# Graph layer 1 in a hand-written order: turned accumulation, 12 target blocks from kept rows instead of 16

## The chip, the cores and the metric

The kernel runs on one core of a Trainium2 chip. Its time is the device time of one execution in microseconds (us), and the number compared is the median of several executions. Before the change the median of 5 runs is 4278.44 us (4270.95 to 4283.33). The engines are named as in the profile: PE multiplies matrices (PEld loads its weights), DVE is the vector engine, ACT the scalar engine, POOL issues the indirect loads ("gathers"), and SP issues the other loads and stores.

## The reference

Four graph layers follow each other over 6250 nodes with 256 features and 100000 edges, sorted by target (`dst`); each ends in a residual and a layer norm. The change is in the second, layer 1. The reference, cut to it:

```
x = _layernorm(x + _L0_gnn_ref(x, edge_index, L0_gnn_W, L0_gnn_b), axis=-1)
x = _layernorm(x + _L1_gnn_ref(x, edge_index, L1_gnn_W1, ...), axis=-1)
x = _layernorm(x + _L2_gnn_ref(x, src, dst, edge_weight, ...), axis=-1)
x = _layernorm(x + _L3_gnn_ref(x, edge_attr_128, edge_index, ...), axis=-1)

def _L1_gnn_ref(h, edge_index, W1, b1, W2, b2, eps, gamma, beta):
    src, dst = (edge_index[0], edge_index[1])
    agg = jax.ops.segment_sum(h[src], dst, num_segments=h.shape[0])
    z = (1.0 + eps) * h + agg
    z = jax.nn.relu(z @ W1 + b1) @ W2 + b2
    r = z + h
    mu = jnp.mean(r, axis=-1, keepdims=True)
    var = jnp.mean(jnp.square(r - mu), axis=-1, keepdims=True)
    ln = (r - mu) * jax.lax.rsqrt(var + LN_EPS) * gamma + beta
    return jax.nn.relu(ln)
```

Targets are drawn as a square, so low node numbers receive many more edges than high ones.

## The kernel before

The nodes are cut into 49 blocks of 128 (`NB`), a block being a tile of 128 partitions x 256 features. The kernel runs in stages, one after the other: a preparation (edge lists and attention scores, 0 to 1020 us of the profiled span), layer 0 (to about 1570), layer 1 (1579.4 to 2317.6), layer 2 (to 3320) and layer 3 (to the end at 4279.5).

Sums over edges are matrix products. Layer 0 leaves each row of x as two halves whose sum is the row (512 values, 256 `hi` and 256 `lo`); most blocks' halves stay in the on-chip memory ("kept rows": `keep`, and `first_rows` for the first 20 blocks, loaded again from `rows`), and all are in the table `rows`. In layer 1 a target block gets its sum over edges in one of two ways.

*Near blocks*, 0 to 15 (`H1` = 16), use kept rows. There are four sweeps of four target blocks each, and each sweep goes over all 49 source blocks: 196 steps. A step makes the one-hot matrices of the edges between a source block and the four targets on DVE (`Pairs`, L1022 `od` by target, L974 through `one_hots` `os` by source), multiplies them on PE (L1284, into `ps_q`) to a 128 x 512 matrix of edge counts, which ACT copies out (L1287, `a_hi`). The next step's `use` multiplies the counts with the source block's kept rows, in eight matmuls of 256 columns (`sum_halves`, L985 and L986, two for each of four targets), which add up in `ps_acc`, laid out target node by feature.

*Far blocks*, 16 to 48, use gathers: 383 tiles of 128 edges, in 76 chunks of up to six. Each tile is a gather of 128 rows of 512 values on POOL (L979, `g`, 8 buffers), and two matmuls (L985, L986) with a one-hot matrix `cs` made on DVE add it to `ps_g`. The chunks are spread evenly over the steps by `want`.

Once a group of four blocks (`GRP`) has its sums, z = (1+eps)x + sum is formed on DVE (L1217), transposed on PE (L357) with a copy on ACT (L358), and `finish` follows: a first product into `ps_b` (L370) with bias and relu on ACT (`y_t`, L1226), the second product (L364), the two sums with b2 and x (L1232, L1233), a layer norm (L344 to L350), gamma and beta (L1235, L1236), relu and the outer residual (L1237), a second layer norm, and the store on SP (L376). A norm takes statistics on DVE (L344, L346), a root on ACT (L348), and a reciprocal and a two-scalar operation on DVE (L349, L350).

Layers 0 and 2 are written in an order fixed by hand (`manual_schedule`). Layer 1 is not: there the framework's scheduler decides the order of the instructions on each engine, while buffer counts bound how far one may run ahead of another.

The preparation loads, for each far block, two columns of the edge list through SP (into `idx_d` and `to`) and makes `loc_d`, the target's place within its block, on DVE. Layer 0's weight `w_raw` is loaded through SP.

Of the kernel before, what the change touches and what calls it, by code (L numbers as in the profile page):

```python
# [7 lines left out]
FT = mybir.dt.float32  # L8
# [42 lines left out]
S_TILES = sum(n for _, _, _, n in STRETCHES)  # L51
TS = NB * S_TILES
S_ROWS = -(-(S_TILES * P * NB + E) // P)
H0, H1, H2, H3 = 24, 16, 9, 3
SURE = 3.5


# [321 lines left out]
def one_plus(k, pool, eps, name):  # L379
    t = bcast_row(k, pool, eps, 1, name)  # L380
    k.nc.vector.tensor_scalar(t, t, 1.0, None, op0=OP.add)
    return t
# [561 lines left out]
def load_block(k, pool, table, b, name="xb", bufs=3):  # L944

    t = pool.tile([P, D], FT, name=name, bufs=bufs)
    n = rows_of(b)
    if n < P:
        k.nc.vector.memset(t, 0.0)
    k.nc.sync.dma_start(t[:n, :], table[b * P:b * P + n, :])  # L950
    return t
# [245 lines left out]
def direct_l1(k, pool, psum, a, rows_at, table, idx_d, loc_d, loc, rel, x_in, out_x):  # L1197


    nc = k.nc  # L1200
    w1 = weight(k, pool, a["L1_gnn_W1"], D, D, "w1")
    w2 = weight(k, pool, a["L1_gnn_W2"], D, D, "w2")
    b1 = column(k, pool, a["L1_gnn_b1"], DK, "b1")
    b2 = bcast_row(k, pool, a["L1_gnn_b2"], D, "b2")
    gamma = bcast_row(k, pool, a["L1_gnn_gamma"], D, "gamma")
    beta = bcast_row(k, pool, a["L1_gnn_beta"], D, "beta")
    eps1 = one_plus(k, pool, a["L1_gnn_eps"], "eps1")

    class Group:
        def __init__(self, b0, n):  # L1210
            self.b0, self.n, self.x = b0, n, {}
            self.z_t = pool.tile([P, DK, GRP * P], FT, name="z_t", bufs=2)

        def add(self, i, ps):
            x = self.x[i] = load_block(k, pool, x_in, self.b0 + i, name="x1", bufs=8)
            z = pool.tile([P, D], FT, name="z1", bufs=2)
            nc.vector.scalar_tensor_tensor(z, x, eps1, ps, op0=OP.mult, op1=OP.add)  # L1217
            transposed(k, self.z_t[:, :, i * P:(i + 1) * P], z)

        def finish(self):  # L1220
            n = self.n
            y_t = pool.tile([P, DK, GRP * P], FT, name="y_t", bufs=2)
            for o in range(DK):
                py = k.psum.tile([P, GRP * P], FT, name="ps_b")
                times_t(k, py[:, :n * P], w1, self.z_t[:, :, :n * P], o)
                nc.scalar.activation(y_t[:, o, :n * P], py[:, :n * P], AF.Relu, bias=b1[:, o:o + 1])  # L1226
            for i in range(n):
                b, x = self.b0 + i, self.x[i]
                pr = k.psum.tile([P, D], FT, name="ps_b")
                times(k, pr, y_t[:, :, i * P:(i + 1) * P], w2)  # L1230
                r = pool.tile([P, D], FT, name="r1", bufs=3)
                nc.vector.tensor_add(r, b2, pr)  # L1232
                nc.vector.tensor_add(r, r, x)  # L1233
                layernorm(k, pool, r, r)
                nc.vector.tensor_mul(r, r, gamma)  # L1235
                nc.vector.tensor_add(r, r, beta)  # L1236
                nc.vector.scalar_tensor_tensor(r, r, 0.0, x, op0=OP.max, op1=OP.add)  # L1237
                layernorm(k, pool, r, r)
                store_block(k, out_x, b, r)

    def far_blocks():
        for b0 in range(H1, NB, GRP):
            g = Group(b0, min(GRP, NB - b0))
            for i in range(g.n):
                b = b0 + i
                ps = psum.tile([P, D], FT, name="ps_g", bufs=2)
                for c0 in range(0, D_TILES[b], CHUNK):
                    m = min(CHUNK, D_TILES[b] - c0)
                    at = D_FIRST[b] + c0
                    s = pool.tile([P, CHUNK, P], F32R, name="cs", bufs=2)  # L1250
                    one_hots(k, s[:, :m, :], loc_d[:, at:at + m])
                    for j in range(m):
                        r = pool.tile([P, W0], FT, name="g", bufs=8)
                        gather(k, r, table, idx_d[:, at + j:at + j + 1])
                        sum_halves(k, ps, s[:, j, :], r, start=(c0 + j == 0), stop=(c0 + j == D_TILES[b] - 1))
                    yield
                g.add(i, ps)
            g.finish()

    far = far_blocks()  # L1260
    n_far = sum(-(-D_TILES[b] // CHUNK) for b in range(H1, NB))
    steps = [(d0, b) for d0 in range(0, H1, 4) for b in range(NB)]
    ones, done, sums = {}, [0], {}

    def open_step(i):
        d0, b = steps[i]
        ones[i] = Pairs(k, pool, b, d0, d0 + 4, loc, rel)

    open_step(0)

    def build(i):
        if i + 1 < len(steps):
            open_step(i + 1)
        d0, b = steps[i]
        p = ones.pop(i)


        pa = psum.tile([P, 4 * P], FT, name="ps_q", bufs=2)
        for m, t in enumerate(p.tiles):
            lo, hi = p.spans[t]  # L1280
            new = next((d for d in range(lo, hi) if p.of(d)[0] == t), hi)
            for d, e in ((lo, new), (new, hi)):
                if d < e:
                    nc.tensor.matmul(pa[:, (d - d0) * P:(e - d0) * P], p.by_source(t), p.by_target(t, d, e - d),  # L1284
                                     start=(m == 0), stop=(m == len(p.tiles) - 1 and e == hi))
        at = pool.tile([P, 4, P], F32R, name="a_hi", bufs=3)
        nc.scalar.copy(at.rearrange("p j s -> p (j s)"), pa)  # L1287
        return at

    def use(i, at):  # L1290
        d0, b = steps[i]
        if b == 0:
            sums[0] = psum.tile([P, 4, D], FT, name="ps_acc", bufs=1)
        for j in range(4):
            n = rows_of(b)
            sum_halves(k, sums[0][:, j, :], at[:n, j, :], rows_at(b)[:n, :], start=(b == 0 and j % 2 == 0),
                       stop=(b == NB - 1 and j % 2 == 1))
        want = (i + 1) * n_far // len(steps)
        while done[0] < want:
            next(far, None)  # L1300
            done[0] += 1
        if b == NB - 1:
            g = Group(d0, 4)
            for j in range(4):
                g.add(j, sums[0][:, j, :])
            g.finish()

    stages(len(steps), 1, build, use)
    for _ in far:
        pass  # L1310


def direct_l2(k, pool, a, hot, idx, loc, rel, scale, x_in, out_rows, out_x, si):
# [595 lines left out]
def prepare(k, a, table0, first, rec, placed, ends, idx_d, loc_d, bad):  # L1909
# [6 lines left out]
    with (  # L1916
# [11 lines left out]
        scatter = Scatter(k, r_s, addr, rec, "scatter")  # L1928
        scores = Scores(k, prep, ps, a["edge_attr_128"], a["L3_gnn_ew_W"], a["L3_gnn_ew_b"], a["L3_gnn_a_W"],
                        r_s[:, :, 3], scatter.columns)  # L1930
        w_raw = weight(k, prep, a["L0_gnn_W"], D, D, "w_raw")
        with tc.tile_pool(name="cols", bufs=1) as cols:
            none = cols.tile([P, TS // 49, 4], FT, name="none")
            for i, v in enumerate((float(NONE), -1.0, 0.0, 0.0)):
# [26 lines left out]
        with tc.tile_pool(name="score", bufs=1) as pool:  # L1961
# [17 lines left out]
            at(NB // 3 + 4, lambda: setattr(scores, "placed", Placed(k, pool, ps, slots, r_s, placed)))  # L1979


            w_t = pool.tile([P, DK, D], FT, name="w_t")
            bias = bcast_row(k, pool, a["L0_gnn_b"], D, "b_row")
            x_ts = {}
# [155 lines left out]
```

## Time and profile before

| | |
|---|---|
| median of 5 runs | 4278.44 us (4270.95 to 4283.33) |
| the profiled execution | 4281.38 us |
| its span | 4279.5 us |
| mean granted PE clock over the span | 0.926 |
| PE busy over the span | 3606.2 us (84%) |
| DVE busy | 2949.8 us (69%) |
| POOL busy | 2737.0 us (64%) |
| ACT busy | 1475.8 us (34%) |
| gathers of layer 1 (L979 with `idx_d`) | 383, 431.5 us busy, mean 1127 ns |

A line of instruction groups is read so: line, engine, operation, what is written `<-` what is read, the number of times, then busy us and mean ns of one, then the idle time of the engine before them and what ended it. "PEclk" is the clock granted to PE, as a share of its full speed. A busy time of PE is larger than the time that its matmuls keep it from others, since they overlap. A line of a timeline has start and duration in us, the engine, the line and the operation, and in brackets the idle time before it with its releaser; SPq is SP's queue.

### The profile page before, as it was taken

Reading aid. Unit: us, or ns where it says so; the run is one execution under the profiler, and the core shown is the slowest. Engines: PE = TensorE matmul, PEld = TensorE weight load, DVE = VectorE, ACT = ScalarE, POOL = GpSimd, SP = SyncE. Lnnn points to the kernel's source line nnn. Section 1 sums busy time; section 2 is a strip of 40 time slices with the busy share of each in tenths; the row PEclk is TensorE's granted clock in tenths of the full one; section 3 lists DMA queues with packets and bytes.
Section 4 is the critical chain, followed back from the end, with each engine's and each line's share of the span. In section 5 each row is a group of like instructions: output and inputs, shape, how many; then the busy total and the mean of one; then the engine's idle time right before and its main releaser. Section 6 shows DMA issues by size and latency. Waiting matters only on the chain. (4 is left out here: it accounts for less than half of the span.)

```text
span 4279.5 us, 70812 instructions
## 1 busy us (share of the span) xinstructions
PE 3606.2 (84%) x23978; PEld 2791.2 (65%) x23988; DVE 2949.8 (69%) x9234; ACT 1475.8 (34%) x3780; POOL 2737.0 (64%) x2685
## 2 busy tenths in 40 slices
PE   7999999984999988988886999999853777777676
PEld 4566666644999977766665777777532565666565
DVE  7787666544777758888887565565286777777775
ACT  1344333331333322222222111111343455555554
POOL 3765655676777757566663777777303777777774
PEclk9999999997999999899998999999997888888888
DMA  4233333325777775456563343343244445444443
GB/s 81 61 88 92 92 87 85 87 54 135 218 211 214 216 228 170 135 170 173 166 184 93 108 108 108 108 109 108 59 111 127 124 133 140 136 137 140 134 139 91
DMA packets 373432, 552.44 MB, mean 129 GB/s; under 512 B 88710, under 2 KB 265064, under 8 KB 372774
## 3 DMA queue, kind: packets, MB, share of 16 engines
q0 software_dynamic: 136064, 353.87, 30.3%
q1 hardware_dynamic: 236998, 193.96, 15.5%
q8 instruction: 193, 3.16, 0.3%
q14 instruction: 177, 1.45, 0.1%
HBM read 486.32 MB, written 62.09 MB: 128 GB/s over the span
## 5 line engine op out<-in xcount | busy, mean ns | idle before, releaser
L979 POOL DMA_INDIRECT g<-rows,idx_s x1032 | 1153.6, 1118 | 393.5 <-issue 239.6
L929 POOL DMA_INDIRECT rec<-r_s,addr x590 | 578.8, 981 | 337.5 <-ACT r_s L829 221.3
L979 POOL DMA_INDIRECT g<-x,idx_s x541 | 560.1, 1035 | 220.9 <-issue 74.3
L979 POOL DMA_INDIRECT g<-rows,idx_d x383 | 431.5, 1127 | 271.9 <-PE ps_g L986 160.6
L825 PE MATMUL ps_b<-ew_w,a_t 128*128 128x257 f32 x1564 | 548.4, 433 | 2.0 <-ACT a_t L815 2.0
L827 DVE SCALAR_TENSOR_TENSOR scr<-ps_b,a 128x256 bf16<-128x256 f32 x782 | 324.9, 422 | 255.8 <-PE ps_b L825 231.5
L1630 PE MATMUL ps_g<-g,s 128*128 128x257 f32 x1374 | 393.0, 454 | 0.0
L1130 PEld LDWEIGHTS <-od 128*128 128x128 bf16 x5947 | 349.2, 98 | 52.9 <-issue 19.8
L1630 PEld LDWEIGHTS ps_g<-g,s 128*128 128x128 f32 x1374 | 315.3, 233 | 59.1
L1138 PE MATMUL ps_g<-g,cs 128*128 128x256 f32 x1082 | 289.6, 394 | 48.6 <-DMA g<-x,idx_s 47.1
L829 ACT ACTIVATE r_s<-ps_b,half 128x1 f32<-128x1 f32 x782 | 201.0, 263 | 360.5 <-DVE scr L827 355.0
L1092 DVE TENSOR_SCALAR od<-iota,rel 128x128 bf16<-128x128 f16 (+9 forms) x780 | 249.4, 400 | 104.1 <-PE ps_q L1130 99.9
L974 DVE TENSOR_TENSOR os<-iota_row,loc_s 128x768 bf16<-128x768 f32 (+3 forms) x294 | 270.9, 921 | 70.6 <-PE ps_q L1284 60.0
L825 PEld LDWEIGHTS ps_b<-ew_w,a_t 128*128 128x128 f32 x1564 | 233.4, 188 | 97.1 <-ACT a_t L815 2.3
L1550 PE MATMUL ps_a<-ident,ep 128*128 128x128 f32 x833 | 163.9, 328 | 148.3 <-DVE ep L1539 89.1
L1133 ACT CAST a_hi<-ps_q 128x512 fp32r<-128x512 f32 x294 | 172.2, 586 | 330.0 <-PE ps_q L1130 319.9
L1133 ACT COPY a_hi<-ps_q 128x512 f32<-128x512 f32 x146 | 69.9, 479 | 593.0 <-PE ps_q L1130 573.4
L985 PE MATMUL ps_g<-g,cs 128*128 128x256 f32 x728 | 232.3, 336 | 46.8 <-DMA g<-rows,idx_d 45.5
L1138 PEld LDWEIGHTS ps_g<-g,cs 128*128 128x128 f32 x1082 | 186.8, 190 | 109.8 <-DMA g<-x,idx_s 89.1
L1287 ACT CAST a_hi<-ps_q 128x512 fp32r<-128x512 f32 x196 | 114.8, 586 | 380.2 <-PE ps_q L1284 379.9
L985 PE MATMUL ps_g<-first_rows,a_hi 128*128 128x256 f32 x980 | 245.7, 283 | 0.0
L986 PE MATMUL ps_g<-first_rows,a_hi 128*128 128x256 f32 x980 | 244.4, 282 | 0.0
(294 smaller groups left out, 8201.0 us busy)
## 6 DMA issues: line engine op xcount, KB each, us to landing
at<-in_edge_attr SPq DMA_DIRECT2D x65, 768.0 KB
edge_row<-node_row SPq DMA_DIRECT2D x49, 544.0 KB
xb<-x SPq DMA_DIRECT2D x144, 128.0 KB
g<-rows,idx_s POOLq DMA_INDIRECT x1032
xb<-in_x SPq DMA_DIRECT2D x96, 128.0 KB
x<-x SPq DMA_DIRECT2D x96, 128.0 KB
rows<-hl SPq DMA_DIRECT2D x47, 256.0 KB
rec<-r_s,addr POOLq DMA_INDIRECT x590
```

What stands on the lines that cost most here:

```text
L825: nc.tensor.matmul(z[:n_e, :], a_t[:, j * P:j * P + n_e], self.w, start=False, stop=True)
L827: nc.vector.scalar_tensor_tensor(scr[:n_e, :], z[:n_e, :D], 0.0, self.a[:n_e, :], op0=OP.max, op1=OP.mult, accum_out=s[:n_e, j:j + 1])
L929: s = nc.gpsimd.indirect_dma_start(out=self.table, out_offset=bass.IndirectOffsetOnAxis(ap=self.addr[:n, c:c + 1], axis=0), in_=self.rec[: ...
L974: k.nc.vector.tensor_tensor(dst, k.iota_row.unsqueeze(1).to_broadcast([P, n, P]), loc.unsqueeze(2).to_broadcast([P, n, P]), op=op)
L979: k.nc.gpsimd.indirect_dma_start(out=dst, out_offset=None, in_=table, in_offset=bass.IndirectOffsetOnAxis(ap=idx, axis=0))
L985: k.nc.tensor.matmul(out, lhs, row[:, :D].bitcast(F32R), start=start, stop=False)
L986: k.nc.tensor.matmul(out, lhs, row[:, D:2 * D].bitcast(F32R), start=False, stop=stop)
L1092: nc.vector.tensor_scalar(od[:, o:o + (hi - lo) * P], k.iota16[:, :(hi - lo) * P], rel[:, s + t:s + t + 1], None, op0=OP.is_equal)
L1130: nc.tensor.matmul(pa[:, j * P:(j + 1) * P], od[:, o:o + P], x[:, t, :], start=(m == 0), stop=(m == len(steps) - 1))
L1133: nc.scalar.copy(a[:, :n, :].rearrange("p j s -> p (j s)"), pa[:, :n * P])
L1138: nc.tensor.matmul(ps, a, row, start=start, stop=stop)
L1630: nc.tensor.matmul(ps, s[:, j, :], g[:, j, :D + 1], start=(j == 0), stop=False)
```

## The change

Layer 1 is written in a fixed order, its near blocks are fewer, and its accumulation is turned.

- `H1` goes from 16 to 12: three sweeps and 147 steps instead of 196. Target blocks 12 to 48 are gathered: 450 tiles in 88 chunks instead of 383 in 76. The preparation loads and prepares the edge lists of four more blocks.
- `ps_acc` is laid out feature by target node. The kept rows are the weights and `a_hi` the moving side: four matmuls of 512 columns a step in place of eight of 256. Near blocks need no z and no transposes: (1+eps)x is added in the accumulation by two small matmuls per block (at source blocks 26 to 29) with `scaled`, the identity times 1+eps, and ACT copies the sum straight to `z_t`. Their x is loaded at source block 18 (`xn`).
- Everything in the layer stands in `manual_schedule`. Iteration i makes the one-hots of step i+1, builds the counts of step i, does one or more pieces of waiting group work (the list `later`), multiplies step i-1, and then uses a chunk if one is due. A chunk's sums (`use_chunk`) are followed by the one-hots and gathers of the next chunk (`open_chunk`). Chunks are due over the first 137 of 148 iterations.
- A group's work is cut in pieces: `first` (first product), then pieces in which `second`, `sums`, `middle` and `end` of successive blocks overlap.
- In the norms gamma, beta and the normalising are folded into operations with one per-partition scalar and one tensor (`scalar_tensor_tensor`); the last normalising goes to ACT as y = r * rs - mean * rs, with a 128 x 1 product `less` on DVE.
- `g` has 11 buffers instead of 8, `ps_g` one instead of two, `ps_b` two.
- `w_raw` is loaded later, after the preparation's first loads.

The diff, without blank lines and with long removed stretches cut (they stand above):

```diff
@@ -51,7 +51,7 @@
 S_TILES = sum(n for _, _, _, n in STRETCHES)
 TS = NB * S_TILES
 S_ROWS = -(-(S_TILES * P * NB + E) // P)
-H0, H1, H2, H3 = 24, 16, 9, 3
+H0, H1, H2, H3 = 24, 12, 9, 3
 SURE = 3.5
@@ -1197,6 +1197,8 @@
 def direct_l1(k, pool, psum, a, rows_at, table, idx_d, loc_d, loc, rel, x_in, out_x):
     nc = k.nc
     w1 = weight(k, pool, a["L1_gnn_W1"], D, D, "w1")
     w2 = weight(k, pool, a["L1_gnn_W2"], D, D, "w2")
@@ -1205,72 +1207,123 @@
     gamma = bcast_row(k, pool, a["L1_gnn_gamma"], D, "gamma")
     beta = bcast_row(k, pool, a["L1_gnn_beta"], D, "beta")
     eps1 = one_plus(k, pool, a["L1_gnn_eps"], "eps1")
+    scaled = pool.tile([P, P], FT, name="scaled")
+    nc.vector.tensor_scalar(scaled, k.ident, eps1, None, op0=OP.mult)
+    later = []
     class Group:
         def __init__(self, b0, n):
-            self.b0, self.n, self.x = b0, n, {}
-            self.z_t = pool.tile([P, DK, GRP * P], FT, name="z_t", bufs=2)
-        def add(self, i, ps):
-            x = self.x[i] = load_block(k, pool, x_in, self.b0 + i, name="x1", bufs=8)
+            self.b0, self.n, self.x, self.r, self.ln, self.pr = b0, n, {}, {}, {}, {}
+            self.z_t = None
+        def inputs(self):
+            if self.z_t is None:
+                self.z_t = pool.tile([P, DK, GRP * P], FT, name="z_t", bufs=2)
+            return self.z_t
+        def load(self, i):
+            near = self.b0 < H1
+            self.x[i] = load_block(k, pool, x_in, self.b0 + i, name="xn" if near else "x1", bufs=4 if near else 8)
+        def turn(self, i, z):
+            transposed(k, self.inputs()[:, :, i * P:(i + 1) * P], z)
+        def first(self):
+            n = self.n
+            self.y_t = pool.tile([P, DK, GRP * P], FT, name="y_t", bufs=2)
+            for o in range(DK):
+                py = psum.tile([P, GRP * P], FT, name="ps_b", bufs=2)
+                times_t(k, py[:, :n * P], w1, self.z_t[:, :, :n * P], o)
+                nc.scalar.activation(self.y_t[:, o, :n * P], py[:, :n * P], AF.Relu, bias=b1[:, o:o + 1])
+        def second(self, i):
+            self.pr[i] = psum.tile([P, GRP * P], FT, name="ps_b", bufs=2)[:, :D]
+            times(k, self.pr[i], self.y_t[:, :, i * P:(i + 1) * P], w2)
+        def sums(self, i):
+            r = self.r[i] = pool.tile([P, D], FT, name="r1", bufs=3)
+            nc.vector.tensor_add(r, b2, self.pr.pop(i))
+            nc.vector.tensor_add(r, r, self.x[i])
+            self.ln[i] = spread(k, pool, r)
+        def middle(self, i):
+            r, (mv, rs) = self.r[i], self.ln[i]
+            nc.vector.reciprocal(rs, rs)
+            nc.vector.scalar_tensor_tensor(r, r, mv[:, 0:1], gamma, op0=OP.subtract, op1=OP.mult)
+            nc.vector.scalar_tensor_tensor(r, r, rs, beta, op0=OP.mult, op1=OP.add)
+            nc.vector.scalar_tensor_tensor(r, r, 0.0, self.x.pop(i), op0=OP.max, op1=OP.add)
+            self.ln[i] = spread(k, pool, r)
+        def end(self, i):
+            mv, rs = self.ln.pop(i)
+            nc.vector.reciprocal(rs, rs)
+            less = pool.tile([P, 1], FT, name="less1", bufs=3)
+            nc.vector.tensor_scalar(less, mv[:, 0:1], rs, -1.0, op0=OP.mult, op1=OP.mult)
+            y = pool.tile([P, D], FT, name="y1", bufs=2)
+            nc.scalar.activation(y, self.r.pop(i), AF.Identity, bias=less, scale=rs)
+            store_block(k, out_x, self.b0 + i, y)
+        def pieces(self):
+            def piece(m):
+                for f, lag in ((self.second, 0), (self.end, 3), (self.middle, 2), (self.sums, 1)):
+                    if 0 <= m - lag < self.n:
+                        f(m - lag)
+            return [self.first] + [lambda m=m: piece(m) for m in range(self.n + 3)]
+    def after(*fs):
+        later.extend(fs)
+    chunks = [(b, c0, min(CHUNK, D_TILES[b] - c0)) for b in range(H1, NB) for c0 in range(0, D_TILES[b], CHUNK)]
+    opened, far_group, far_sum = {}, {}, {}
+    def open_chunk(c):
+        b, c0, m = chunks[c]
+        at = D_FIRST[b] + c0
+        if c0 == 0:
+            i = (b - H1) % GRP
+            if i == 0:
+                far_group[b] = Group(b, min(GRP, NB - b))
+            far_group[b - i].load(i)
+        s = pool.tile([P, CHUNK, P], F32R, name="cs", bufs=2)
+        one_hots(k, s[:, :m, :], loc_d[:, at:at + m])
+        rows = []
+        for j in range(m):
+            rows.append(pool.tile([P, W0], FT, name="g", bufs=11))
+            gather(k, rows[-1], table, idx_d[:, at + j:at + j + 1])
+        opened[c] = s, rows
+    def use_chunk(c):
+        b, c0, m = chunks[c]
+        s, rows = opened.pop(c)
+        if c0 == 0:
+            far_sum[b] = psum.tile([P, D], FT, name="ps_g", bufs=1)
+        ps = far_sum[b]
+        for j in range(m):
+            sum_halves(k, ps, s[:, j, :], rows[j], start=(c0 + j == 0), stop=(c0 + j == D_TILES[b] - 1))
+        if c0 + m == D_TILES[b]:
+            i = (b - H1) % GRP
+            g = far_group[b - i]
             z = pool.tile([P, D], FT, name="z1", bufs=2)
-            nc.vector.scalar_tensor_tensor(z, x, eps1, ps, op0=OP.mult, op1=OP.add)
...
-    n_far = sum(-(-D_TILES[b] // CHUNK) for b in range(H1, NB))
+            nc.vector.scalar_tensor_tensor(z, g.x[i], eps1, far_sum.pop(b), op0=OP.mult, op1=OP.add)
+            after(lambda: g.turn(i, z))
+            if i == g.n - 1:
+                after(*g.pieces())
+        if c + 1 < len(chunks):
+            open_chunk(c + 1)
     steps = [(d0, b) for d0 in range(0, H1, 4) for b in range(NB)]
-    ones, done, sums = {}, [0], {}
+    ones, sums, near_group, made = {}, {}, {}, {}
     def open_step(i):
         d0, b = steps[i]
         ones[i] = Pairs(k, pool, b, d0, d0 + 4, loc, rel)
-    open_step(0)
     def build(i):
-        if i + 1 < len(steps):
-            open_step(i + 1)
         d0, b = steps[i]
         p = ones.pop(i)
@@ -1283,31 +1336,56 @@
                 if d < e:
                     nc.tensor.matmul(pa[:, (d - d0) * P:(e - d0) * P], p.by_source(t), p.by_target(t, d, e - d),
                                      start=(m == 0), stop=(m == len(p.tiles) - 1 and e == hi))
-        at = pool.tile([P, 4, P], F32R, name="a_hi", bufs=3)
-        nc.scalar.copy(at.rearrange("p j s -> p (j s)"), pa)
-        return at
-    def use(i, at):
+        at = made[i] = pool.tile([P, 4 * P], F32R, name="a_hi", bufs=3)
+        nc.scalar.copy(at, pa)
+    def use(i):
         d0, b = steps[i]
+        at, n = made.pop(i), rows_of(b)
         if b == 0:
-            sums[0] = psum.tile([P, 4, D], FT, name="ps_acc", bufs=1)
...
-            done[0] += 1
+            sums[0] = psum.tile([P, DK, 4 * P], FT, name="ps_acc", bufs=1)
+        acc = sums[0]
+        for o in range(DK):
+            for part in range(2):
+                row = rows_at(b)[:n, part * D + o * P:part * D + (o + 1) * P]
+                nc.tensor.matmul(acc[:, o, :], row.bitcast(F32R), at[:n, :], start=(b == 0 and part == 0),
+                                 stop=(b == NB - 1 and part == 1))
+        g = near_group.get(d0)
+        if b == 18:
+            g = near_group[d0] = Group(d0, 4)
+            for j in range(4):
+                g.load(j)
+        if 26 <= b < 30:
+            j = b - 26
+            for o in range(DK):
+                nc.tensor.matmul(acc[:, o, j * P:(j + 1) * P], g.x[j][:, o * P:(o + 1) * P], scaled, start=False,
+                                 stop=False)
         if b == NB - 1:
-            g = Group(d0, 4)
...
-        pass
+            for o in range(DK):
+                nc.scalar.copy(g.inputs()[:, o, :], acc[:, o, :])
+            after(*g.pieces())
+    with k.tc.manual_schedule():
+        open_step(0)
+        open_chunk(0)
+        done = 0
+        for i in range(len(steps) + 1):
+            if i + 1 < len(steps):
+                open_step(i + 1)
+            if i < len(steps):
+                build(i)
+            for _ in range(1 + len(later) // 5):
+                if later:
+                    later.pop(0)()
+            if i:
+                use(i - 1)
+            want = min(len(chunks), (i + 1) * len(chunks) // (len(steps) - 10))
+            while done < want:
+                use_chunk(done)
+                done += 1
+        while later:
+            later.pop(0)()
 def direct_l2(k, pool, a, hot, idx, loc, rel, scale, x_in, out_rows, out_x, si):
@@ -1928,7 +2006,6 @@
         scatter = Scatter(k, r_s, addr, rec, "scatter")
         scores = Scores(k, prep, ps, a["edge_attr_128"], a["L3_gnn_ew_W"], a["L3_gnn_ew_b"], a["L3_gnn_a_W"],
                         r_s[:, :, 3], scatter.columns)
-        w_raw = weight(k, prep, a["L0_gnn_W"], D, D, "w_raw")
         with tc.tile_pool(name="cols", bufs=1) as cols:
             none = cols.tile([P, TS // 49, 4], FT, name="none")
             for i, v in enumerate((float(NONE), -1.0, 0.0, 0.0)):
@@ -1979,6 +2056,7 @@
             at(NB // 3 + 4, lambda: setattr(scores, "placed", Placed(k, pool, ps, slots, r_s, placed)))
+            w_raw = weight(k, pool, a["L0_gnn_W"], D, D, "w_raw")
             w_t = pool.tile([P, DK, D], FT, name="w_t")
             bias = bcast_row(k, pool, a["L0_gnn_b"], D, "b_row")
             x_ts = {}
```

`spread(k, pool, x)` takes the statistics of a norm (DVE) and the root (ACT) and returns mean and root; the caller forms the reciprocal. In the changed file the lines of layer 1 are L1337 (counts), L1340 (`a_hi`), L1351 (accumulation), L1362 (`scaled`), L1366 (copies to `z_t`), L1312 (z of far blocks), L1248 and L1249 (`sums`), L1254 to L1257 (`middle`) and L1262 to L1266 (`end`).

More of the change, by code (lines that the diff above doesn't have):

```diff
@@ L1207, in direct_l1 @@
     eps1 = one_plus(k, pool, a["L1_gnn_eps"], "eps1")
+    scaled = pool.tile([P, P], FT, name="scaled")
+    nc.vector.tensor_scalar(scaled, k.ident, eps1, None, op0=OP.mult)
+    later = []
     class Group:
         def __init__(self, b0, n):
-            self.b0, self.n, self.x = b0, n, {}
-            self.z_t = pool.tile([P, DK, GRP * P], FT, name="z_t", bufs=2)
-        def add(self, i, ps):
-            x = self.x[i] = load_block(k, pool, x_in, self.b0 + i, name="x1", bufs=8)
-            z = pool.tile([P, D], FT, name="z1", bufs=2)
-            nc.vector.scalar_tensor_tensor(z, x, eps1, ps, op0=OP.mult, op1=OP.add)
-            transposed(k, self.z_t[:, :, i * P:(i + 1) * P], z)
@@ L1220, in finish @@
[L1220 to L1258, printed above, removed]
@@ L1260, in direct_l1 @@
-    far = far_blocks()
-    n_far = sum(-(-D_TILES[b] // CHUNK) for b in range(H1, NB))
+            self.b0, self.n, self.x, self.r, self.ln, self.pr = b0, n, {}, {}, {}, {}
[7 more added lines that the diff above has]
+            self.x[i] = load_block(k, pool, x_in, self.b0 + i, name="xn" if near else "x1", bufs=4 if near else 8)
@@ L1285, in build @@
                                      start=(m == 0), stop=(m == len(p.tiles) - 1 and e == hi))
-        at = pool.tile([P, 4, P], F32R, name="a_hi", bufs=3)
-        nc.scalar.copy(at.rearrange("p j s -> p (j s)"), pa)
-        return at
-    def use(i, at):
+        at = made[i] = pool.tile([P, 4 * P], F32R, name="a_hi", bufs=3)
+        nc.scalar.copy(at, pa)
+    def use(i):
         d0, b = steps[i]
+        at, n = made.pop(i), rows_of(b)
         if b == 0:
-            sums[0] = psum.tile([P, 4, D], FT, name="ps_acc", bufs=1)
[L1294 to L1300, printed above, removed]
-            done[0] += 1
-        if b == NB - 1:
-            g = Group(d0, 4)
-            for j in range(4):
-                g.add(j, sums[0][:, j, :])
-            g.finish()
@@ L1308, in direct_l1 @@
-    stages(len(steps), 1, build, use)
-    for _ in far:
-        pass
+            sums[0] = psum.tile([P, DK, 4 * P], FT, name="ps_acc", bufs=1)
[6 more added lines that the diff above has]
+        g = near_group.get(d0)
```

## The prediction

> **What bounds the kernel now.** The chain of waits on the page is of no help (every share in it is 0%), so I went by stages: first the busy time of each engine in windows whose borders are the first and last instruction of a layer, then the groups and waits of layer 1 alone, then the timeline at its two ends.
>
> ```profile
> core 0: us, PE busy (x) PEld busy (x) DVE busy (x) ACT busy (x) POOL busy (x), PEclk, DMA share, GB/s
> 1020.00:1570.00 550.00, 545.96 (x5918) 533.03 (x5915) 377.00 (x857) 202.94 (x393) 381.10 (x337) 1.00 0.70 213
> 1579.40:2317.60 738.20, 619.10 (x3944) 485.12 (x3954) 599.97 (x1894) 178.47 (x372) 431.49 (x383) 0.91 0.56 161
> 2318.00:3055.00 737.00, 683.61 (x5215) 559.97 (x5215) 430.42 (x1100) 99.40 (x218) 560.10 (x541) 0.99 0.39 106
> ```
>
> The middle line is layer 1, the only stage whose inner work changes: 738.2 us. No engine is full. PE is busy 84% at a granted clock of 0.91, DVE 81%, POOL 58%. So two engines near full wait on each other, and POOL has room.
>
> ```profile
> L979 POOL DMA_INDIRECT g<-rows,idx_d x383 | 431.5, 1127 | 271.9 <-PE ps_g L986 160.6 <-issue 57.9 <-DMA first_rows<-rows 21.7
> L985 PE MATMUL ps_acc<-keep,a_hi 128*128 128x256 f32 x464 | 144.3, 333 | 14.2 <-ACT a_hi L1287 13.7
> L1022 DVE TENSOR_SCALAR od<-iota,rel 128x512 bf16<-128x512 f16 x294 | 96.3, 354 | 0.0
> L974 DVE TENSOR_TENSOR os<-iota_row,loc_s 128x512 bf16<-128x512 f32 x99 | 67.2, 679 | 15.5 <-PE ps_q L1284 15.3
> L974 DVE TENSOR_TENSOR cs<-iota_row,loc_d 128x768 fp32r<-128x768 f32 x48 | 45.4, 948 | 18.5 <-PE ps_g L986 18.5
> L350 DVE TENSOR_SCALAR r<-r,ln_mv,ln_rs 128x256 f32<-128x256 f32 x98 | 40.5, 418 | 0.3
> ```
>
> These groups give the prices. The first says who holds POOL: its gather waits 160.6 us for PE to have summed an earlier tile, so that one of 8 buffers comes free.
>
> ```profile
> POOL g L979 <- PE ps_g L986: 160.6, 88, 16.6
> DVE os L974 <- PE ps_q L1284: 60.0, 36, 6.3
> PEld ps_g L985 <- DMA g<-rows,idx_d: 56.2, 50, 2.6
> PEld ps_acc L985 <- ACT a_hi L1287: 44.2, 58, 3.1
> PE ps_q L1284 <- DVE od L1022: 32.0, 36, 14.1
> ```
>
> The waits (total us, times, longest) go round: DVE for PE, PE for DVE, ACT and gathers. The layer advances by 196 steps, and what a step costs DVE and PE sets the end.
>
> ```profile
> 1710.48 1.12 POOL L979 DMA_INDIRECT g<-rows,idx_d  x1 [0.30 <-issue]
> 1728.24 1.69 POOL L979 DMA_INDIRECT g<-rows,idx_d  x1 [16.64 <-PE ps_g L986]
> ```
>
> Two neighbours on POOL's timeline: a gather costs its duration plus 0.30 us of issue, and a hole of 16.64 us shows that POOL is not what is short.
>
> ```profile
> 2225.41 0.32 SPq L376 DMA_DIRECT2D x<-r  x1
> 2270.45 0.37 SPq L1782 DMA_DIRECT2D hot<-x  x1
> ...
> 2275.22 0.32 SPq L376 DMA_DIRECT2D x<-r  x1
> ...
> 2283.19 30.57 SPq L376 DMA_DIRECT2D x<-r  x8
> ```
>
> At the layer's end SP's queue stands 45 us (2225.4 to 2270.5) before a load for layer 2 that needs the last sum. Between the last matmul into ps_acc (2270.3) and the first work of layer 2 (2317.6), 47 us, DVE finishes nine blocks.
>
> **The change part by part.**
>
> *POOL.* 383 gathers become 450. All 383 took 431.5 us, 1.127 each, with 0.305 of issue: 1.432, so 548 us of the 738. 450 × 1.432 = 644 us, from the first at 1580.3 to 2224.7. The price has two ends. The shortest gather, which overlaps no DVE operation with two SBUF inputs, takes 0.945; those that overlap one average 1.213 (253 of the 383), and layer 2's 541 average 1.035 with a lighter DVE. From below, layer 2's 1.339 with issue: 603 us. From above, the stretch (0.182) grows as DVE's two-input work packs more densely, by 0.75/0.60 to 0.23: 1.48, or 666 us. I take 1.432, the nearest row.
>
> The trace first: gathers beside two-input DVE operations are 1.213 against 0.945 us. The Trainium skill ("GPSIMD Engine Reference", 8. Key points) says that GpSimd shares its SBUF interfaces with VectorE and contends with instructions that have two SBUF inputs; that speaks against this change, which lengthens POOL's chain and leaves cs, os and the norms on DVE. It gives no price; if every gather took the contended 1.213 + 0.305, the chain would be 683 us instead of 644.
>
> *DVE.* Removed: a sweep of 49 os at 0.679 (33 us) and its 196 od at about 0.32, between the 256- and the 512-wide form, 0.281 and 0.354 (63). The norms' folding turns two L350, gamma and beta into two operations with three inputs and one on ACT: two fewer per block, 2 × 0.415 × 49 = 41. Sixteen near z at 0.470 leave, four far ones come: 5.6. Added: one-hots for 67 tiles at 0.948/6 (10.6), 49 of the small `less` at 0.15 (7.4). Net −125: 600 to 475, over 148 iterations 3.2 us; chained operations start 0.46 apart where they last 0.41, ten a block, which makes 3.4.
>
> *PE.* At full clock matmuls of 256 columns follow each other in 0.12 us (0.21 at half clock, as around 1711), 512 bf16 in 0.216, 512 full-width float in 0.43. Before: ps_acc 196 × 8 × 0.12 = 188, gathered sums 92, builds 130, products and transposes 94: 504. After: 147 × 4 × 0.216 = 127, 450 × 2 × 0.12 = 108, builds 91, the rest 94: 420, or 2.84 us an iteration, 3.1 at the clock of 0.91. The eight small matmuls a sweep that add (1+eps)x are in it (24 × 0.11). ACT loses 49 a_hi (0.586 each) and gains 49 normalisations: it is at 24%.
>
> *Who sets the pace then.* Only the first 137 of 148 iterations carry chunks, so POOL needs 644/137 = 4.70 us an iteration, above DVE's 3.4 and PE's 3.1. The fixed order puts the chunk's sums last in an iteration, so PE now stands there until rows land; behind it on PE are the next build and a piece of group work, and DVE, whose one-hots have two buffers, waits one step later. With 11 buffers for chunks of up to 6, POOL runs ahead through this. At three sweep ends the single ps_acc must be copied by ACT (2 × 0.586 and the handing over, 1.7): 5 us, charged in full.
>
> *After the last gather* (2229.7): landing and summing 3.3 (the longest wait for rows, 2.6, and six matmuls); 11 iterations without chunks at 0.68 for os and four od at 0.27, 1.75 each: 19.3; DVE's pieces for some three blocks of the last far groups, each 1.45 (sums), 2.0 (middle) and 0.3 (end): 11.3. Then, behind the last step, ACT's two copies of ps_acc (1.2) and its casts for layer 2 (1.7 + 1.7): 4.6; the two products with their relu, about 6.4; four blocks' pieces, 15: 26 together. The store's landing 4.1, as before. 2229.7 + 3.3 + 19.3 + 11.3 + 26 + 4.1 = 2293.7, against 2317.6: −23.9.
>
> *Edits at nothing.* Eight more edge loads on SP and four small DVE subtractions for four more blocks, and w_raw issued some 70 us later: all in the first 1020 us, where PE is busy 926 and sets the pace. Without that cover: 8 × 0.37 = 3 us of SP and 0.6 of DVE. x loads of near blocks come at source block 18 and are used at 26, eight iterations or 37 us ahead; stores on SP wait for ACT's last step, with later x loads behind them, and these are needed a chunk (7 us) later at the earliest against 2 to 4 of landing. Layers 2 and 3 are shifted, unchanged.
>
> *Sum.* The profiled execution took 4281.4 (span 4279.5): 4281.4 − 23.9 = 4257.5. It lies 2.9 above the median 4278.44, so on the median 4254.6, I say **4255**.
>
> **The rivals.**
>
> *B, gathers less stretched.* DVE has a fifth less to do, and layer 2, with less DVE per us, has 1.339. Then 603 us: 42 less, 4213. For it: the stretch comes from DVE. Against: the removed work is half od, which has one input; two-input work falls less than the stage's time.
>
> *C, the order couples the engines (slower).* Before, 60 and 32 us of mutual waits stood in a scheduler's order; in a fixed one PE's sums stand before its next build, and a PE that waits for rows falls to half clock (0.21 us spacing). If half of PE's 3.1 us is in series with DVE's 3.4, an iteration is 3.4 + 1.55 = 4.95, above POOL's 4.70: 148 × 4.95 = 733, the layer's steps end at 2313, with 30 of tail and store 2343: +25, 4304. It decides once the mean iteration passes (2317.6 − 30 − 1580)/148 = 4.78 us, only 2% above POOL's own pace. For it: that narrowness. Against: 11 buffers instead of 8, and DVE is one step ahead.
>
> The row first: 0.12 us spacing at 1905, 0.21 at 1711 in the same layer. The Trainium skill ("TensorE: Matmul & The Clock Gate", Part 1) has the clock fall to half after an idle window of some 3.4 us and rise again with sustained work, which speaks against a change that makes PE wait more; all at half clock, PE's iteration would be an estimated 5.7 us.
>
> *D, nothing seen.* POOL's chain comes out at 666 and the tail as before: −2, within 8.6 us (0.2%, about what this kernel's measurement can tell from no change).
>
> **How the numbers follow.** The main case 0.50, with its own range 4232 (tail and half of B's gain) to 4277 (666 us); B 0.11; C 0.34; D 0.05. Faster by over 8.6 us: 0.40 of the main case and B, 0.51. Same: 0.09 of the main case, D, 0.04 of C: 0.18. Slower: the rest of C and a little of the main case's top, 0.31. The range takes in B's 4213 and C's 4304 with some of C's tail: 4211 to 4316.
>
> **What would show it.** Right: POOL's gathers of layer 1 number 450, idle for ps_g nearly gone, issue-spaced from 1580 to about 2225; DVE about 475 us busy; layer 2 starts near 2294. B shows as a mean gather near 1.035. C shows as POOL idle for PE's sums again and DVE os/PE od waits above 100 us in sum, a granted clock below 0.85. What makes it wrong: a mean iteration above 4.78 us, or a longer tail.

## The result and the profile after

The changed kernel takes 4286.77 us (median of 28 runs, 4277.43 to 4296.24), the kernel before 4278.59 (48 runs): a ratio of 1.0018, 95% interval [1.0012, 1.0024]. It is 8 us slower, where 24 us faster was forecast. (In the runs of e5 to e8 below the granted clock was lower, 0.84 to 0.85 over the profiled spans against 0.91 to 0.93 elsewhere, and the kernel before took 4964.5 us, against 4271.2 on the same chip in the runs of e9 to e12, so for those four only ratios are given.) The profiled execution took 4285.68 us, span 4283.8, 4.3 above that of before. Layer 2 begins 4.4 us later, and after it nothing differs, so the whole difference lies in layer 1.

The busy times in windows for the changed kernel: layer 0, layer 1 up to its last gather, the rest of layer 1, and the first part of layer 2.

```profile
core 0: us, PE busy (x) PEld busy (x) DVE busy (x) ACT busy (x) POOL busy (x), PEclk, DMA share, GB/s
1020.00:1570.00 550.00, 545.30 (x5907) 532.38 (x5904) 377.02 (x857) 202.76 (x393) 375.85 (x337) 1.00 0.70 213
1578.00:2252.00 674.00, 518.91 (x2753) 384.19 (x2758) 480.19 (x1437) 150.11 (x317) 495.48 (x450) 0.87 0.68 197
2252.00:2321.80 69.80, 41.47 (x179) 26.89 (x178) 51.99 (x163) 24.21 (x49) 0.66 (x1) 0.82 0.17 51
2321.80:3059.00 737.20, 682.77 (x5215) 558.36 (x5215) 430.03 (x1101) 99.07 (x217) 559.61 (x541) 0.99 0.39 106
```

Layers 0 and 2 are as they were. In layer 1 no engine is full: DVE is busy 480 + 52 = 532 us instead of 600, POOL 496 instead of 431, and PE's granted clock is 0.87 up to the last gather (0.92 before, over 1580.3 to 2262.0) and 0.82 behind it (0.72 before).

The groups of the changed kernel that answer to those of before (POOL's gathers, `od`, the wide `cs`), and the norms' new operations:

```profile
L979 POOL DMA_INDIRECT g<-rows,idx_d x450 | 496.1, 1103 | 198.5 <-PE ps_g L986 65.9 <-issue 64.4 <-DMA first_rows<-rows 21.4
L1022 DVE TENSOR_SCALAR od<-iota,rel 128x512 bf16<-128x512 f16 x148 | 47.0, 345 | 0.0
L974 DVE TENSOR_TENSOR cs<-iota_row,loc_d 128x768 fp32r<-128x768 f32 x57 | 53.9, 946 | 0.0
L1256 DVE SCALAR_TENSOR_TENSOR r<-r,ln_rs,beta 128x256 f32<-128x256 f32 x49 | 24.0, 489 | 1.7
L1264 DVE TENSOR_SCALAR less<-ln_mv,ln_rs 128x1 f32<-128x1 f32 x49 | 10.5, 214 | 1.7
```

And its waits (total us, times, longest):

```profile
DVE z L1312 <- PE ps_g L986: 80.7, 23, 10.0
POOL g L979 <- PE ps_g L986: 65.9, 88, 8.8
PE ps_q L1337 <- DVE od L1022: 59.8, 22, 13.5
DVE os L974 <- PE ps_q L1337: 52.5, 16, 8.6
```

POOL waits much less for PE's sums than before (65.9 for 160.6), but not little: of its idle time between gathers, what goes beyond the 0.305 us of issue sums to 40 us, in 13 holes. DVE's wait in front of z (L1312) is new in size (11.1 us before): DVE stands there until a far block's last sum is in. That `ps_g` has one buffer instead of two shows nowhere: of PE's waits in layer 1 none at `ps_g` is for z.

One of the larger holes, seen from POOL and from PE on the changed kernel's timeline:

```profile
1851.66 1.07 POOL L979 DMA_INDIRECT g<-rows,idx_d  x1 [0.30 <-issue]
1859.90 0.95 POOL L979 DMA_INDIRECT g<-rows,idx_d  x1 [7.17 <-PE ps_g L986]
```

```profile
1845.90 0.83 PE L1337 MATMUL ps_q<-od,os 128*128 128x128 bf16 x7
1846.54 1.17 PE L1351 MATMUL ps_acc<-a_hi,keep 128*128 128x512 f32 x4
1855.83 1.56 PE L1337 MATMUL ps_q<-od,os 128*128 128x128 bf16 x7 [8.12 <-DVE od L1022]
```

POOL stops for 7.17 us because no buffer has been summed; PE, which would sum, stands at the next build and waits 8.12 us for `od`. What DVE did meanwhile:

```profile
1844.97 1.14 DVE L1022 TENSOR_SCALAR od<-iota,rel 128x128 bf16<-128x128 f16 x5
1846.02 0.15 DVE L1262 RECIPROCAL ln_rs<-ln_rs 128x1 f32<-128x1 f32 x1
...
1846.40 0.47 DVE L1255 SCALAR_TENSOR_TENSOR r<-r,ln_mv,gamma 128x256 f32<-128x256 f32 x1
...
1850.47 0.47 DVE L1255 SCALAR_TENSOR_TENSOR r<-r,ln_mv,gamma 128x256 f32<-128x256 f32 x1
...
1853.95 0.92 DVE L974 TENSOR_TENSOR cs<-iota_row,loc_d 128x768 fp32r<-128x768 f32 x1
1854.80 0.82 DVE L974 TENSOR_TENSOR os<-iota_row,loc_s 128x640 bf16<-128x640 f32 x1
1855.53 1.13 DVE L1022 TENSOR_SCALAR od<-iota,rel 128x128 bf16<-128x128 f16 x5
```

Between two sets of `od`, from 1846.0 to 1854.0, stand two pieces of group work (two `middle`, L1255), 8 us in one iteration. The rule `1 + len(later) // 5` puts two or three pieces into an iteration as soon as a group is complete, while other iterations have none. In the 15 us before each hole and in it, group work (the lines of `sums`, `middle` and `end` with their statistics, durations added up) takes 41 to 69% of DVE's time at ten of the 13, against 23% over layer 1's stretch of gathers.

### The profile page after: what moved, and what is told of

It is laid out like the page before. It is cut to its first block, busy times and chain, and to the rows that moved or that the text cites. A ratio compares the mean times of both kernels' runs of the same rounds, so it can differ in the third digit from the quotient of the medians.

```text
span 4283.8 us, 68535 instructions
## 1 busy us (share of the span) xinstructions
PE 3547.5 (83%) x22964; PEld 2712.0 (63%) x22969; DVE 2882.5 (67%) x8945; ACT 1472.7 (34%) x3774; POOL 2793.3 (65%) x2752
## 3 DMA queue, kind: packets, MB, share of 16 engines
q1 hardware_dynamic: 238150, 194.03, 15.5%
## 5 line engine op out<-in xcount | busy, mean ns | idle before, releaser
L979 POOL DMA_INDIRECT g<-rows,idx_d x450 | 496.1, 1103 | 198.5 <-PE ps_g L986 65.9
L1708 PE MATMUL ps_g<-g,s 128*128 128x257 f32 x1374 | 405.5, 465 | 0.0
L1138 PE MATMUL ps_g<-g,cs 128*128 128x256 f32 x1082 | 290.1, 395 | 49.4 <-DMA g<-x,idx_s 48.2
L985 PE MATMUL ps_g<-g,cs 128*128 128x256 f32 x795 | 259.1, 341 | 85.5 <-DMA g<-rows,idx_d 72.3
L1133 ACT CAST a_hi<-ps_q 128x512 fp32r<-128x512 f32 x294 | 172.5, 587 | 329.1 <-PE ps_q L1130 325.3
L974 DVE TENSOR_TENSOR os<-iota_row,loc_s 128x768 bf16<-128x768 f32 (+4 forms) x245 | 237.8, 971 | 61.9 <-PE ps_q L1337 52.5
L1628 PE MATMUL ps_a<-ident,ep 128*128 128x128 f32 x833 | 154.2, 313 | 151.1 <-DVE ep L1617 101.2
L1138 PEld LDWEIGHTS ps_g<-g,cs 128*128 128x128 f32 x1082 | 186.2, 190 | 111.8 <-DMA g<-x,idx_s 89.4
L985 PE MATMUL ps_g<-first_rows,a_hi 128*128 128x256 f32 x980 | 246.2, 284 | 0.0
L985 PEld LDWEIGHTS ps_g<-g,cs 128*128 128x128 f32 x795 | 159.6, 201 | 114.6 <-DMA g<-rows,idx_d 92.6
```

Of the source, the lines that this page charges most:

```text
L979: k.nc.gpsimd.indirect_dma_start(out=dst, out_offset=None, in_=table, in_offset=bass.IndirectOffsetOnAxis(ap=idx, axis=0))
L985: k.nc.tensor.matmul(out, lhs, row[:, :D].bitcast(F32R), start=start, stop=False)
L1133: nc.scalar.copy(a[:, :n, :].rearrange("p j s -> p (j s)"), pa[:, :n * P])
L1138: nc.tensor.matmul(ps, a, row, start=start, stop=stop)
L1628: nc.tensor.transpose(pe[:, i * P:(i + 1) * P], made[b, "ep"][:, t:t + 1].to_broadcast([P, P]), k.ident)
L1708: nc.tensor.matmul(ps, s[:, j, :], g[:, j, :D + 1], start=(j == 0), stop=False)
```

## The experiments

Two theories stood against each other. Theory P: POOL's gathers are the bound up to the last one, and bursts of group work make it stall. Theory S: DVE and PE in series set every iteration, and POOL only waits. Ratios are to the kernel before, run beside each version, with their 95% interval. In the tables behind the experiments "holes" are POOL's idle time between layer 1's gathers beyond 0.305 us each, added up from the trace of the profiled execution.

**e1: the fixed order with 16 blocks from kept rows.**

```diff
-H0, H1, H2, H3 = 24, 12, 9, 3
+H0, H1, H2, H3 = 24, 16, 9, 3
```

> The changed kernel with 16 target blocks from kept rows again (four sweeps, 383 gathers); the fixed order, the turned sums, the folded norms and the 11 buffers stay. Theory P (in the changed kernel POOL's chain of gathers is the bound up to the last gather, with 40 us of holes where pieces of group work come in bursts): with 383 gathers of 1.41 us POOL needs 540 us, so DVE's own work (about 3.4 us for each of 197 iterations, 670 us) decides and layer 1 ends 10 to 60 us earlier than before the change, 4220 to 4270. Theory S (DVE and PE in series set each iteration at 4.9 us, POOL only waits for them): 197 iterations take some 960 us, +200 us or more.

Measured: 4307.15 us, 1.0080 [1.0063, 1.0096]. Both theories miss: S by far (no iteration costs 4.9 us when there are 197 of them), P because the holes are not 40 us here but 143, as in the scheduler's order. So the parts of the change pull apart: at 16 blocks the fixed order, together with the turned sums, the folded norms and the new buffer counts, costs 0.8%, and the sweep less, within it, pays (1.0080 to 1.0018). Which of the parts that stand together here costs, this run doesn't say.

**e2: the scheduler's order with 12 blocks.**

```diff
-H0, H1, H2, H3 = 24, 16, 9, 3
+H0, H1, H2, H3 = 24, 12, 9, 3
...
-        w_raw = weight(k, prep, a["L0_gnn_W"], D, D, "w_raw")
...
+            w_raw = weight(k, pool, a["L0_gnn_W"], D, D, "w_raw")
```

> The kernel before with 12 target blocks from kept rows, and the later load of w_raw that makes room for it; the scheduler's order, the sums as they were, 8 buffers. 450 gathers of 1.43 us are 644 us. Theory P: POOL is then the bound and its holes (134 us before, in 8 buffers) stay in part, 50 to 130 us: the last gather ends between 2275 and 2355, and the layer 55 us later as before, so between 4290 and 4370. If a sweep less is simply a quarter of the work less, the layer takes 3/4 of its steps and ends at POOL's 2224 + 55, about 4240.

Measured: 4285.81 us, 1.0024 [1.0013, 1.0036]. A sweep less does not shorten the layer by itself: the last gather ends at 2257.9 (before: 2262.0), since POOL now has 450 gathers with 60 us of holes. PE, with less work, waits more for gathered rows (L985 for `g`: 85.5 us instead of 45.5). The time lies a little under P's 4290; the gathers came out at 1.074 instead of 1.127, which is 24 us over 450. Without any fixed order, then, a sweep less gives what the whole change gives, 1.0018, to within the intervals.

**e3: chunks due over all 148 iterations.**

```diff
-            want = min(len(chunks), (i + 1) * len(chunks) // (len(steps) - 10))
+            want = min(len(chunks), (i + 1) * len(chunks) // len(steps))
```

> The changed kernel with its chunks due over all 148 iterations instead of the first 137. Theory P: the last gather still ends near 2252, the steps now end with it, and only the last groups' pieces follow, some 40 us instead of 69: 20 to 30 us less, about 4262. Theory S: each iteration takes 4.9 us also at the end, 11 more of them at that pace instead of 2.9: 15 to 20 us more, about 4303.

Measured: 4267.88 us, 0.9986 [0.9976, 0.9997], some 14 us under the changed kernel by the ratios. From the last gather to layer 2's first it takes 54.6 us instead of 69.9. This is P's direction, but less than its 20 to 30 us, and the tail is longer than its 40. S, which wanted 16 us more, falls here: the iterations cost what POOL costs while POOL has gathers, and less where it has none.

**e4: group work spread out.**

```diff
-            after(lambda: g.turn(i, z))
+            turns.append(lambda: g.turn(i, z))
...
-            for _ in range(1 + len(later) // 5):
+            while turns:
+                turns.pop(0)()
+            for _ in range(1 + len(later) // 12):
```

> The changed kernel with group work spread out: turns (the transposes of a far block) are done at once, and of the other pieces one an iteration comes (two from a queue of 12) instead of one more for every five that wait. Theory P: the 13 holes of POOL (40 us) all lie where two or three pieces stand in one iteration, 4 us of DVE each ahead of the next one-hots; with one an iteration at least half of them goes, 15 to 30 us less, 4257 to 4272. Theory S: DVE's work is the same and so is the time, within 8 us of 4287.

Measured: 4254.71 us, 0.9954 [0.9939, 0.997]: 27 us under the changed kernel by the ratios, with the same work on every engine. (The expectation's "all" was too much: three of the 13 holes stand beside little group work.) The gathers in e4:

```profile
L979 POOL DMA_INDIRECT g<-rows,idx_d x450 | 486.9, 1082 | 179.3 <-issue 64.0 <-PE ps_g L986 48.4 <-DMA g<-rows,idx_d 21.9
```

The wait for PE's sums is 48.4 us instead of 65.9, the holes 21.7 instead of 40.4, and the last gather ends at 2222.2, where the prediction had 2224.7. Of the 30.5 us by which it ends sooner, 18.7 are holes, 9.2 shorter gathers (1.082 for 1.103) and 2.5 an earlier start; beside e9 below, the changed kernel in a profile with gathers of 1.084, 25.7 of 27.1 us are holes.

**e5 to e8: e3 and e4 together; e1 with e4's edit; bursts raised; 8 gather buffers.** Their kernels are those of e10, e12, e11 and e13, which ask the same again.

> The two edits of e3 and e4 together: chunks due over all 148 iterations and group work spread out. e4 ended its gathers at 2222 and layer 1 some 71 us later; e3's tail was 54 us. If POOL's chain and what follows its last gather add up, the two gains add: about 4235 (15 to 25 us under e4). If e3's gain came only from fewer holes, it is already in e4, and the time is e4's 4255 within 8 us.

> e1 (16 target blocks from kept rows, fixed order) with the group work spread out as in e4. e1 had 143 us of holes on POOL and took 4307. Theory P (bursts of group work are what the fixed order costs): 25 to 60 us less, 4247 to 4282. Rival (the fixed order as such costs it, each iteration tying DVE, PE and ACT together): at least 4297.

> The changed kernel with one more piece of group work an iteration for every two that wait, instead of every five: the suspected cost raised, the work the same. Theory P: POOL's holes grow from 40 us to 70 or 100, the time by 20 to 50 us, 4307 to 4337. Rival (the holes come from elsewhere, as from the wait for a far block's sum): unchanged within 8 us of 4287.

> The changed kernel with 8 gather buffers instead of 11. Each buffer is 1.4 us of reserve on POOL's chain, so three less deepen each of 13 holes by up to 4.2 us and open new ones: theory P says 30 to 60 us more, 4317 to 4347. If the reserve didn't matter (POOL waits for something that lasts however far ahead it is), within 8 us of 4287.

Measured, as ratios: e5 0.9958 [0.993, 0.9986], e6 0.9972 [0.9945, 0.9999], e7 1.017 [1.0126, 1.0213], e8 1.0068 [1.0042, 1.0095]. The changed kernel was not run beside these four, so the gains and losses that the expectations name can't be read from them; in order they agree with e10 to e13, but e6 lies under the kernel before and e12 doesn't.

**e9: the changed kernel again**, as a measure for e10 to e12.

> The changed kernel itself, as the common measure for the three beside it on whatever chip these land on (e5 to e8 ran on a chip where the kernel before takes 4964 us): 8 us above the kernel before, with some 40 us of holes on POOL, if the chip is like the first.

Measured: 4279.17 us, 1.0015 [1.0005, 1.0025], with 47 us of holes.

**e10: e3 and e4 together.**

> As e5. Gains that add: 40 to 55 us under the changed kernel of this call, last gather near 2222 and 48 us to the end of the layer. Gains that overlap: 32 us under it, like e4.

Measured: 4235.09 us, 0.9915 [0.9893, 0.9938]; 44 us under e9 and 36 under the kernel before. The gains add, and this version beats both kernels. Its layer 1 up to the last gather and behind it, in windows:

```profile
1575.20:2214.10 638.90, 512.63 (x2853) 381.76 (x2853) 495.56 (x1488) 155.80 (x328) 487.86 (x450) 0.90 0.70 208
2214.10:2269.80 55.70, 22.69 (x85) 15.08 (x83) 36.55 (x113) 17.85 (x39) 0.00 (x0) 0.72 0.20 61
```

638.9 us for 450 gathers are 1.42 each, of which 1.084 + 0.305 = 1.389 is the gathers' own: POOL is now all but gapless. The end was longer (56 us) than the 48 expected.

**e11: bursts raised.**

```diff
-            for _ in range(1 + len(later) // 5):
+            for _ in range(1 + len(later) // 2):
```

> As e7: one more piece an iteration for every two that wait. Theory P: holes of POOL well above those of the changed kernel, 20 to 50 us over it. Rival: within 8 us of it.

Measured: 4343.28 us, 1.0162 [1.014, 1.0185], 64 us over the changed kernel: in P's direction, and more than its range. The waits of e11:

```profile
POOL g L979 <- PE ps_g L986: 133.3, 83, 14.7
DVE z L1312 <- PE ps_g L986: 113.8, 32, 9.9
...
PE ps_q L1337 <- DVE od L1022: 79.1, 23, 13.7
```

Against the changed kernel POOL's wait for sums has doubled, and PE's wait for `od` has grown from 59.8 to 79.1. Nothing but the order of the same pieces differs.

**e12: e1 with the group work spread out.**

> As e6: e1 with the group work spread out. Theory P: 25 to 60 us under e1's ratio to the kernel before (1.008), so 0.994 to 1.002 of it. Rival, the fixed order as such: at least 1.005.

Measured: 4277.95 us, 1.0013 [1.0002, 1.0023], 0.0067 under e1: P's range, the rival's 1.005 not reached. Smoothed, the fixed order at 16 blocks, with the turned sums and folded norms, is level with the scheduler's order without them; it gains nothing of itself.

**e13 and e14: 8 and 13 gather buffers in the changed kernel.**

```diff
-            rows.append(pool.tile([P, W0], FT, name="g", bufs=11))
+            rows.append(pool.tile([P, W0], FT, name="g", bufs=8))
```

> As e8: 8 gather buffers instead of 11 in the changed kernel. Three buffers are 4.2 us of reserve. If the holes are what the reserve doesn't cover of each burst, 13 holes deepen by up to 4.2 us and more open: 30 to 60 us over the changed kernel, a ratio to the kernel before of 1.009 to 1.016. If the reserve is without weight, 1.0015 as e9.

```diff
-            self.x[i] = load_block(k, pool, x_in, self.b0 + i, name="xn" if near else "x1", bufs=4 if near else 8)
+            self.x[i] = load_block(k, pool, x_in, self.b0 + i, name="xn" if near else "x1", bufs=4 if near else 6)
...
-            rows.append(pool.tile([P, W0], FT, name="g", bufs=11))
+            rows.append(pool.tile([P, W0], FT, name="g", bufs=13))
...
-        at = made[i] = pool.tile([P, 4 * P], F32R, name="a_hi", bufs=3)
+        at = made[i] = pool.tile([P, 4 * P], F32R, name="a_hi", bufs=2)
```

> 13 gather buffers; the room comes from two buffers of x of far blocks (8 to 6) and one of a_hi (3 to 2). Two buffers are 2.8 us of reserve for 13 to 17 holes of 1 to 9 us: 20 to 30 us less, a ratio of 0.994 to 0.997, if the reserve is what counts and neither x nor a_hi becomes a wait. If a_hi or x do, the ratio stays at 1.0015 or above, and the waits name them.

Measured: e13 4320.08 us, 1.0100 [1.0084, 1.0115]; e14 4274.37 us, 0.9994 [0.9984, 1.0003]. The loss moves both ways with the reserve: 83 us of holes with 8 buffers, 40 to 47 with 11, 34 with 13. e14 gains 9 us, under half of what was expected. Its holes explain why: those at 1844.1, 1870.6 and 1883.7 are 7.17, 4.58 and 5.39 us deep, and e9 has 7.16, 4.50 and 5.39 at the corresponding places (1848.4, 1874.9, 1887.9). It looks as if no reserve builds up again within a train of loaded iterations: two more buffers shrink the train's first holes (e9 has two of 2.16 us there beyond the issue, e14 one of 1.54) and leave the later ones as they are. Whether two buffers of `a_hi` or six of x also cost something wasn't separated.

```
(us)                      ratio    gathers       holes  last gather ends  layer 2's first gather
before                    1        383 x 1.127   134    2262.0            2318.4
changed                   1.0018   450 x 1.103    40    2252.7            2322.6
changed again (e9)        1.0015   450 x 1.084    47    2249.3            2319.2
fixed order, 16 (e1)      1.0080   383 x 1.123   143    2267.3            2347.5
  and spread out (e12)    1.0013   383 x 1.122   123    2246.0            2320.3
scheduler, 12 (e2)        1.0024   450 x 1.074    60    2257.9            2321.3
chunks to the end (e3)    0.9986   450 x 1.088    42    2244.3            2298.9
spread out (e4)           0.9954   450 x 1.082    22    2222.2            2294.5
both (e10)                0.9915   450 x 1.084    14    2214.1            2270.4
bursts raised (e11)       1.0162   450 x 1.092   109    2316.6            2392.8
8 buffers (e13)           1.0100   450 x 1.075    83    2279.7            2352.8
13 buffers (e14)          0.9994   450 x 1.091    34    2237.1            2311.5
```

## Why the prediction was wrong

The step that failed is this one: "With 11 buffers for chunks of up to 6, POOL runs ahead through this", and with it the 5 us charged for POOL's holes. They were 40 us. The prediction divided POOL's and DVE's work evenly over the iterations (4.70 against 3.4 us) and took the difference for a margin. The work is not even. An iteration with two pieces of group work holds 10 to 11 us of DVE (1845 to 1855.5 above), and several follow each other, while the reserve of 11 buffers is 15.5 us of gathers (11 × 1.408). e4 and e11 change nothing but how the pieces are spread and move the time by −27 and +64 us; e13 and e14 change the reserve: with 8 buffers the time grows (1.0100), with 13 it falls (0.9994).

Point by point, on the profiled execution:

- *POOL's price*, 1.432 us a gather: 1.103 + 0.305 = 1.408, 11 us less than forecast over 450, and between its two ends, 1.339 and 1.48.
- *POOL's holes*, 5 us: 40, so 35 more. The term that decided.
- *Landing and the last sums*, 3.3 us: 9 (the last gather ends at 2252.7, the last gathered matmul at 2261.7). PE still had two iterations and group products ahead of them. Under-sized by 5.5.
- *From there to layer 2*, 60.7 us: 60.3. Up to the last sum into `ps_acc` (2294.0) it is 32.3 where 30.6 was forecast, behind it 28.0 where 30.1 was; these terms came out as worked out, and e3 shows that part of them needn't stand there at all.
- *The sum*: −23.9 − 11 + 35 + 5.5 and −1 for an earlier start make +5; measured 2322.0 against 2317.6, +4.4.
- *DVE*, 475 us: 532. Two terms were off. The operations with three inputs take 0.466 and 0.489 rather than 0.415, and `less` 0.214 rather than 0.15, so the folding saved 24 us (81.2 for L350, L1235 and L1236 before, 57.3 for L1255, L1256 and L1264 after) instead of 34. And neighbouring operations overlap in the record: the busy times of DVE's groups in layer 1 sum to 725 us before and 619 after, 106 less, while the engine's own fell by 68. What is taken off by durations counts the overlap too. This made the margin smaller, 3.6 us busy an iteration instead of 3.2 (3.4 with the gaps); by itself it does not reach 4.70.
- *PE*, 3.1 us an iteration: its durations overlap, so this can't be read off. The turned matmuls start 0.237 us apart (median) where 0.216 was taken.
- *Edits at nothing*: right. Layer 1's first gather starts at 1579.4 (before: 1580.3), so the four more blocks' edge lists and the later w_raw cost nothing that shows.

Of the rivals, C named the point from which it decides, a mean of 4.78 us over all 148 iterations, and this was passed: (2294.0 − 1579.4)/148 = 4.83. (The prediction set 4.78 beside POOL's 4.70 and saw 2% between them, but 4.70 is over 137 iterations. Its own steps end at 2263.6, which over 148 makes 4.62, so the margin was 3.5%.) Up to the last gather an iteration took 673.3/137 = 4.91. C's coupling did occur, PE standing before its next build for `od` and POOL behind it for PE's sums, but in the bursts. DVE and PE in series in every iteration is not what happened; e4, with the same engines' work and the same order of steps, needs (2222.2 − 1576.9)/137 = 4.71, the pace that the main case had. C's sign, waits of DVE's `os` and PE's `od` above 100 us in sum, turned out to tell nothing: they sum to 112 (52.5 + 59.8) in the changed kernel and to 115 (65.7 + 49.1) in e4, which is 27 us faster. Its other sign, a granted clock below 0.85, was not reached (0.87). D's chain of 666 us is close to the measured 673, for another reason: it had longer gathers, and the gathers were shorter. B's 1.035 was not reached by any run (1.074 to 1.103 for 450).

What was right, that POOL becomes the bound and that the change can gain, is shown by e10. Why the fixed order, with all that came with it, gains nothing over the scheduler's order at 16 blocks (e12: 1.0013) nor, in the form that was predicted, at 12 (1.0018 against e2's 1.0024, with intervals that overlap) was not taken apart further; at 16 its holes stay at 123 us when smoothed, so there it is not the pieces alone that hold POOL.

## What to carry to other kernels

When work is moved onto an engine with room, its new chain can be taken for the bound only if what frees its buffers is even: compare the reserve (buffers times the price of one) with the longest stretch of other work that stands ahead of the engine that frees them, not with the mean. A rule that works off a queue faster the longer it gets makes such stretches; one piece an iteration did the same work 27 us sooner. And work that needs the bound engine should not stop eleven iterations before the end.

## What the runs showed of the hardware

A gather that overlaps a DVE operation with two tensor inputs (TENSOR_TENSOR and SCALAR_TENSOR_TENSOR together) took 1.170 us on average in the changed kernel, 314 of the 450, and 0.948 otherwise; in e10 1.122 and 0.955. (A few of these operations read one input from PSUM.) This agrees with the Trainium skill ("GPSIMD Engine Reference", 8. Key points), by which GpSimd shares its SBUF interfaces with VectorE and contends with instructions that have two SBUF inputs. But the mean did not grow with the density of this work, as feared: counted so, the kernel before had 1.173 us for 303 of its 383 gathers, and the changed kernel gave 1.103 over all gathers in one profile and 1.084 in another (e9), so differences of 2% in it are not the edit's.

The granted clock over layer 1's stretch of gathers was 0.92 before, 0.87 in the changed kernel, 0.88 in e4 and 0.90 in e10, with PE busy 87, 77, 78 and 80% of it. Behind the last gather it was 0.72, 0.82, 0.83 and 0.72, with PE busy 50, 59, 61 and 41%. The Trainium skill ("TensorE: Matmul & The Clock Gate", Part 1) has the clock fall in idle windows, and the rows agree: where PE is busy less, its clock is lower. What the lower clock costs in time no run separates; e4 and e10 are faster than the kernel before with a lower clock in this stretch.
